# Folding two biases of a feed-forward block into its weight products, and sharing eight copies between two engines

## The chip, the cores and the metric

The kernel runs on one core of a Trainium2 chip. The metric is the device time of one execution in microseconds (us). The core has five kinds of workers that run at the same time and wait for one another through semaphores: TensorE (PE, with its weight loads shown apart as PEld), VectorE (DVE), ScalarE (ACT), GpSimd (POOL), and the queue of SyncE (SP), which issues the transfers (DMA). All data is float32.

## The reference

Four residual steps on tokens x (2 x 1024 x 256) with a context of 2 x 64 x 256. Only the second step changes; the first matters for one detail.

```python
x = x + L0_xattn(layernorm(x), ctx)      # 8 heads of 64, 4 windows; q,k,v products, softmax, Wo, bo
x = x + L0_ffn(layernorm(x))             # below
x = x + L1_xattn(layernorm(x), ctx)      # 16 heads of 16, sigmoid
x = x + L1_ffn(x)                        # soft mixture: logits, two softmaxes, 8 experts, gelu

def L0_ffn(x):                           # 8 groups of 256 tokens, each with its own weights
    xg = x.reshape(8, 256, 256)
    h1 = einsum('gmh,goh->gmo', xg, W1) + b1[:, None, :]     # 1024 wide, no activation
    h2 = einsum('gmo,gho->gmh', h1, W2) + b2[:, None, :]
```

There is nothing between the two products of L0_ffn, and the layernorm has neither scale nor shift, so that the 256 numbers of a normed token add up to zero.

## The kernel before, in words

Tokens stand in four quads of 512 (`xq[q]`, four tiles of 128 rows). Weights of the feed-forward groups come as one tensor `wff`: for each group, on each of 128 partitions, eight rows (oc) of 2 x 256 numbers, W1 beside W2 transposed. `load_group(g)` (L836) reads one group, 2 MB, into one of three buffers `wg`; group 0 comes in five pieces, group 1 in two.

`product(g)` (L852) multiplies the two weights of a group into one 256 x 256 matrix: 16 matmuls (each is two MATMUL instructions in the profile, so 32) into a PSUM bank `pmt`, copied to `mt` (L867). `bias_rows(g)` (L870) makes b1 W2: for groups 0 and 1 on PE with b1 broadcast to 32 columns (`pp`, L878, and one DVE step, L885), for the others as eight sums on DVE (L890). They add up in `b2z`, whose row 0 got b2 by DMA and whose other rows were set to zero. `bias(g)` (L894) multiplies b2z by ones, so that the sum over the partitions stands on all of them (`pbs`, L896), and copies it to `bs` (L898). `norm_ff(q)` (L904) norms a quad (moments on DVE, rstd on POOL at L124 and L125, the scaling `hn` on DVE at L819) and transposes it on PE (L133) with copies to `hT` (L134). `feed_forward(q)` (L908) adds `bs` to the tokens on POOL (L912), multiplies hT by mt (`po`, L918) and adds the result to the tokens on DVE (L925).

Around them stands the first attention: `pk` and `pv` (L991, L1004) make keys and values of the context. The values go from PSUM to a block layout `vblk` in eight copies of 64 x 128 on ACT (L1014). `pwk` (L1025) and `pvw` (L1043) fold keys and values with the projections; their banks come from the same four as pk's and pv's. `weigh(q)` makes scores (`psc`, L1068), maxima (L1078), differences (L1080), exponentials on ACT (L1085), sums and weights (L1087, L1090); `turn_weights` transposes them (`pat`, L1101, copy `atT` on ACT, L1103); `attend` multiplies by the folded values (`po`, L1114) and adds to the tokens (L1122).

The program text gives a priority, not the order: each engine's order is laid out when the kernel is built, from what is ready by a plan of the times, and runs in that order. The calls from L1126 on interleave `weigh`, `attend`, `product`, `bias`, `bias_rows`, `norm_ff` and `feed_forward`. Operations written as `nc.any` get ACT or DVE in that plan. SP's queue holds the loads in one order as well: group 4's load (L841) can start only when the buffer of group 1 has no more readers, and w1s and se (`load_layer1`, the weights of later steps) follow on the same queue.

From about 116 us the second attention runs (L1259 to L1369), then the soft mixture, which the change doesn't touch.

Of the kernel before, what the change touches and what calls it, by code (L numbers as in the profile page):

```python
# [9 lines left out]
FP = mybir.dt.float32  # L10
AF = mybir.ActivationFunctionType
ALU = mybir.AluOpType
# [3 lines left out]
P = 128  # L16
B = 2
S = 1024
D = 256
DC = D // P  # L20
# [13 lines left out]
NG, FF = 8, 1024  # L34
OC = FF // P
# [17 lines left out]
def tile_kernel(  # L53
# [19 lines left out]
    nc = tc.nc  # L73
# [9 lines left out]
    def bank(name, side=0):  # L83
        return ps[side].tile([P, 512], FP, tag="bank", name=name)
# [3 lines left out]
    ones = const.tile([P, P], FP, name="ones")  # L88
# [710 lines left out]
    with (  # L799
# [7 lines left out]
        ggb = w1p.tile([P, 2, D], FP, name="ggb")  # L807

        NCT, NPE = DC * B * NK, DC * NK
        fr = w1p.tile([P, NCT + NPE + NG * OC], FP, name="fr")  # L810
        ctxd = fr[:, 0:NCT].rearrange("p (c b s) -> p c b s", c=DC, b=B)
        pes = fr[:, NCT : NCT + NPE].rearrange("p (c s) -> p c s", c=DC)
        b1s = fr[:, NCT + NPE :].rearrange("p (g c) -> p g c", g=NG)

        def normed(xt, name):
            mv, rstd = moments(xt, name)
            hn = lnp.tile([P, QT, D], FP, tag="hn", name=f"hn_{name}")
            for t in range(QT):
                nc.vector.tensor_scalar(  # L819
                    hn[:, t, :], xt[:, t, :], mv[:, t, 0:1], rstd[:, t : t + 1],  # L820
                    ALU.subtract, ALU.mult,
                )
            return hn

        def layernorm(xt, name, side=0, out=nc.any.tensor_copy):
            hn = normed(xt, name)
            hT = lnp.tile([P, DC, QN], FP, tag="hT", name=f"hT_{name}")
            transposed(hn, hT, name, side, out)
            return hT

        wide = ExitStack()
        wff = wide.enter_context(tc.tile_pool(name="wff", bufs=3))
        ffc = wide.enter_context(tc.tile_pool(name="ffc", bufs=1))
        weights = {}

        def load_group(g, parts=(OC,)):  # L836

            wg = wff.tile([P, OC, 2, D], FP, tag="wg", name=f"wg_{g}")
            i = 0
            for n in parts:  # L840
                nc.sync.dma_start(out=wg[:, i : i + n], in_=wff_in[g, :, i : i + n])  # L841
                i += n
            weights[g] = wg[:, :, 0, :], wg[:, :, 1, :]


        b2z = ffc.tile([P, NG, D], FP, name="b2z")
        bo_bc = ffc.tile([P, D], FP, name="bo_bc")


        mts, bss = [], []  # L850

        def product(g):  # L852
            if g not in weights:
                load_group(g)
            w1g, w2g = weights[g]
            pm = bank(f"pmt_{g}", 1)
            for oc in range(OC):
                for hc in range(DC):
                    nc.tensor.matmul(  # L859
                        pm[:, ts(hc, D)],  # L860
                        lhsT=w1g[:, oc, ts(hc, P)],
                        rhs=w2g[:, oc, :],
                        start=(oc == 0 and hc == 0),
                        stop=(oc == OC - 1 and hc == DC - 1),
                    )
            mt = ffc.tile([P, DC, D], FP, name=f"mt_{g}")
            nc.any.tensor_copy(mt, pm.rearrange("p (c n) -> p c n", c=DC))  # L867
            mts.append(mt)

        def bias_rows(g):  # L870

            acc = b2z[:, g, :]
            if g < 2:

                pp = bank(f"pp0_{g}", 1)
                for oc in range(OC):
                    j = oc % 4
                    nc.tensor.matmul(  # L878
                        pp[ds(32 * j, 32), 0:D],
                        lhsT=b1s[:, g, oc : oc + 1].to_broadcast([P, 32]),  # L880
                        rhs=weights[g][1][:, oc, :],
                        start=(oc < 4),
                        stop=(oc >= 4),
                    )
                nc.vector.scalar_tensor_tensor(  # L885
                    acc, pp[:, 0:D], 1.0 / 32.0, acc, ALU.mult, ALU.add
                )
                return
            for oc in range(OC):
                nc.vector.scalar_tensor_tensor(  # L890
                    acc, weights[g][1][:, oc, :], b1s[:, g, oc : oc + 1], acc, ALU.mult, ALU.add
                )

        def bias(g):  # L894
            pb = bank(f"pbs_{g}", 1)
            nc.tensor.matmul(pb[:, 0:D], lhsT=ones, rhs=b2z[:, g, :], start=True, stop=True)  # L896
            bs = ffc.tile([P, D], FP, name=f"bs_{g}")
            nc.any.tensor_copy(bs, pb[:, 0:D])  # L898
            bss.append(bs)


        hTfs = {}
# [5 lines left out]
        def feed_forward(q, side=0):  # L908
            for i in range(QN // GN):
                g = q * (QN // GN) + i  # L910
                xg = xq[q][:, ts(i, 2), :]
                nc.gpsimd.tensor_tensor(  # L912
                    xg, xg, bss[g].unsqueeze(1).to_broadcast([P, 2, D]), ALU.add
                )
                po = bank(f"po_{g}", side)
                for t in range(2):
                    for dc in range(DC):
                        nc.tensor.matmul(  # L918
                            po[:, ts(t, D)],
                            lhsT=hTfs[q][:, dc, ds(i * GN + t * P, P)],  # L920
                            rhs=mts[g][:, dc, :],
                            start=(dc == 0),
                            stop=(dc == DC - 1),
                        )
                nc.vector.tensor_tensor(  # L925
                    xg, xg, po.rearrange("p (t d) -> p t d", t=2), ALU.add
                )
# [7 lines left out]
        with tc.tile_pool(name="p0", bufs=1) as p0, tc.tile_pool(name="a0", bufs=2) as a0:  # L935

            wk0s = p0.tile([P, DC, H0 * DH0], FP, name="wk0s")
            wv0s = p0.tile([P, DC, H0 * DH0], FP, name="wv0s")
            wq0s = p0.tile([P, C0, D], FP, name="wq0s")
# [6 lines left out]
                nc.sync.dma_start(out=xTs[q], in_=xT[q])  # L946
                nc.sync.dma_start(out=xq[q], in_=x[q])

            nc.gpsimd.memset(b2z, 0.0)
            load_group(0, (1, 1, 2, 2, 2))  # L950
            for t_, s_ in (
                (fr, front), (wk0s, wk0), (wq0s, wq0), (wv0s, wv0), (b2z[0:1], b2.unsqueeze(0)),
                (wo0s, wo0), (bo_bc, bo0.partition_broadcast(P)),
            ):
                nc.sync.dma_start(out=t_, in_=s_)
# [33 lines left out]
            for c in range(C0):  # L989
                for dc in range(DC):  # L990
                    nc.tensor.matmul(  # L991
                        pk[:, ts(c, P)],
                        lhsT=wk0s[:, dc, ts(c, P)],
                        rhs=hcT[:, dc].rearrange("p b j -> p (b j)"),
                        start=(dc == 0),
                        stop=(dc == DC - 1),
# [5 lines left out]
            for c in range(C0):  # L1002
                for dc in range(DC):
                    nc.tensor.matmul(  # L1004
                        pv[:, ts(c, P)],
                        lhsT=wv0s[:, dc, ts(c, P)],
                        rhs=hcT[:, dc].rearrange("p b j -> p (b j)"),
                        start=(dc == 0),
                        stop=(dc == DC - 1),
                    )  # L1010
            for c in range(C0):
                for e in range(2):
                    r = slice(e * DH0, (e + 1) * DH0)
                    nc.scalar.copy(  # L1014
                        vblk[r, c, :, e, :],
                        pv[r, ts(c, P)].rearrange("p (w j) -> p w j", j=KJ),
                    )

            wk = p0.tile([P, DC, NBW, H0 * KJ], FP, name="wk")
            for dc in range(DC):  # L1020
                pws = [bank(f"pwk_{dc}_{e}") for e in range(2)]
                for c in range(C0):
                    for e in range(2):
# [3 lines left out]
                            lhsT=wq0s[r, c, ts(dc, P)],  # L1027
                            rhs=kT[r, c, :],
                            start=True,
                            stop=True,  # L1030
# [8 lines left out]
            for g in range(NBW // 2):  # L1039
                pw = bank(f"pvw_{g}")  # L1040
                for i in range(2):
                    for c in range(C0):
                        nc.tensor.matmul(  # L1043
                            pw[ds(32 * c, 32), ts(i, D)],
                            lhsT=vblk[:, c, 2 * g + i].rearrange("p e j -> p (e j)"),
                            rhs=wo0s[:, c, :],
                            start=True,
                            stop=True,
# [75 lines left out]
                    )  # L1124

            weigh(0)  # L1126
            bias_rows(0)
            product(1)
            turn_weights(0)
            weigh(1)  # L1130
            attend(0)
            product(2)
            bias(0)
            bias_rows(1)
            weigh(2)
            attend(1)
            norm_ff(0)
            product(3)
            bias(1)
            bias_rows(2)  # L1140
            feed_forward(0)
            weigh(3)
            attend(2)
            product(4)
            bias(2)
            bias_rows(3)
            load_layer1()
            norm_ff(1)
            attend(3)
        product(5)  # L1150
        bias(3)
        bias_rows(4)
        feed_forward(1)
        product(6)
        bias(4)
        bias_rows(5)
        norm_ff(2)
        bias(5)
        bias_rows(6)
        feed_forward(2)  # L1160
        bias(6)

        with (
            tc.tile_pool(name="a1c", bufs=1, side="right") as a1c,
# [35 lines left out]
            for c in range(C1):  # L1200
                for dc in range(DC):
                    nc.tensor.matmul(
                        pk[:, ts(c, P)],
                        lhsT=wk1s[:, dc, ts(c, P)],
                        rhs=ctxd[:, dc],
# [82 lines left out]
            norm_ff(NQ - 1)  # L1288
            norm_queries(1)
            norm_queries(2)  # L1290
            bias_rows(7)


            vsum = a1c.tile([P, C1, B], FP, name="vsum")
# [14 lines left out]
                vsum, pvs[:, 0 : C1 * B].rearrange("p (c b) -> p c b", c=C1), 0.5, None, ALU.mult  # L1309
            )  # L1310
            queries(0)
            bias(7)
            turn_slot_rows(0)
            work = ExitStack()
            for q in range(NQ):
# [204 lines left out]
```

## Time and profile before

| what | value |
|---|---|
| median of 3 runs | 430.95 us (430.89 to 431.24) |
| the profiled execution | 430.34 us, of which the span in the profile is 428.6 |
| PE, PEld, DVE, ACT, POOL busy in the span | 421.4, 313.4, 336.9, 111.2, 81.6 us |
| L859, the products of the weights | 256 MATMULs, 57.9 us busy |
| L890, sums of b1 W2 on DVE | 48, 24.5 us busy |
| L896 and L878, bias matmuls on PE | 16 and 32 MATMULs |
| L912, adds of the bias on POOL | 8, 10.4 us busy |
| granted TensorE clock | 1.0 throughout |

A group of the profile is one line, one engine and one operation: tiles written and read, partitions x elements, the number, then busy time, the mean of one in ns, and the idle time of the engine just ahead of them with what ended it. The chain that ended last is followed back from the last instruction, at each step to what released it. Matmuls overlap in the records, so the busy time of PE is more than the work it has; the distance from one start to the next tells the pace.

### The profile page before, as it was taken

Reading aid. Unit: us, or ns where it says so; the run is one execution under the profiler, and the core shown is the slowest. Engines: PE = TensorE matmul, PEld = TensorE weight load, DVE = VectorE, ACT = ScalarE, POOL = GpSimd, SP = SyncE. Lnnn points to the kernel's source line nnn. Section 1 sums busy time; section 2 is a strip of 40 time slices with the busy share of each in tenths; the row PEclk is TensorE's granted clock in tenths of the full one; section 3 lists DMA queues with packets and bytes.
Section 4 is the critical chain, followed back from the end, with each engine's and each line's share of the span. In section 5 each row is a group of like instructions: output and inputs, shape, how many; then the busy total and the mean of one; then the engine's idle time right before and its main releaser. Section 6 shows DMA issues by size and latency. Waiting matters only on the chain.

```text
span 428.6 us, 6368 instructions
## 1 busy us (share of the span) xinstructions
PE 421.4 (98%) x2318; PEld 313.4 (73%) x2318; DVE 336.9 (79%) x753; ACT 111.2 (26%) x210; POOL 81.6 (19%) x83
## 2 busy tenths in 40 slices
PE   8999999999999999999999999999999999999997
PEld 7788797888644445444478844799998874499996
DVE  0587989899767788997768989995994489785956
ACT  1212224203444431433570455400000003520000
POOL 3012232225212220200975920000000000000000
PEclk9999999999999999999999999999999999999999
DMA  8997695420462431321043663551012665620002
GB/s 275 401 419 314 242 377 203 186 98 2 154 197 99 81 44 29 45 30 21 0 161 148 114 96 58 79 81 20 0 38 76 134 116 89 97 44 1 2 2 98
DMA packets 99281, 50.03 MB, mean 117 GB/s; under 512 B 87857, under 2 KB 94385, under 8 KB 97841
## 3 DMA queue, kind: packets, MB, share of 16 engines
q1 hardware_dynamic: 99250, 49.63, 41.5%
q8 instruction: 18, 0.29, 0.3%
q14 instruction: 13, 0.11, 0.1%
HBM read 32.74 MB, written 6.30 MB: 91 GB/s over the span
## 4 chain that ended last, share of the span: by engine, by line
PE 79%; DVE 13%; SPq 2%; DMA 2%; issue 1%; ACT 1%; POOL 1%; DVEq 0%; ACTq 0%
PE psl L409 13%; PE pc L586 12%; PE pp L586 11%; PE pmh L511 10%; PE pmt L859 9%; PE pl L256 7%; PE pq L1259 3%; PE po L918 2%; DVE b2z L890 2%; SPq L158 2%; PE pf L1273 2%; PE psg L1329 1%; PE poT L1361 1%; DMA wg<-in_wff_dram 1%; DVE lg L264 1%
## 5 line engine op out<-in xcount | busy, mean ns | idle before, releaser
L859 PE MATMUL pmt<-wg 128*128 128x256 f32 x256 | 57.9, 382 | 0.4 <-DMA wg<-in_wff_dram 0.4
L409 PE MATMUL psl<-xh,lg 128*128 128x258 f32 x256 | 56.8, 380 | 0.0
L256 PE MATMUL pl<-seT,xhT 128*128 128x512 f32 x128 | 56.1, 594 | 0.2 <-DVE rmax L275 0.2
L859 PEld LDWEIGHTS pmt<-wg 128*128 128x128 f32 x256 | 48.5, 192 | 7.3 <-DMA wg<-in_wff_dram 0.8
L409 PEld LDWEIGHTS psl<-xh,lg 128*128 128x128 f32 x256 | 48.2, 190 | 7.4 <-issue 0.5
L256 PEld LDWEIGHTS pl<-seT,xhT 128*128 128x128 f32 x128 | 24.1, 190 | 29.2 <-issue 25.7
L395 POOL TENSOR_TENSOR lg<-lg,mb 128x1024 f32<-128x1024 f32 x13 | 33.2, 2607 | 26.8 <-ACT mb L203 25.3
L586 PEld LDWEIGHTS pp<-ms,mh 128*128 128x128 f32 x256 | 29.4, 192 | 1.3 <-issue 0.7
L586 PE MATMUL pp<-ms,mh 128*128 128x128 f32 x256 | 30.0, 276 | 0.1
L279 ACT ACTIVATE ec<-lg,nm 128x1024 f32<-128x1024 f32 x16 | 18.4, 1149 | 39.8 <-DVE nm L264 39.8
L890 DVE SCALAR_TENSOR_TENSOR b2z<-wg,fr,b2z 128x256 f32<-128x256 f32 x48 | 24.5, 513 | 0.3
L521 ACT ACTIVATE mh<-mh 128x512 f32<-128x512 f32 x32 | 19.2, 627 | 20.8 <-DVE mh L557 19.2
L511 PE MATMUL pmh<-slT,ms 128*128 128x512 f32 x48 | 24.2, 592 | 0.0
L586 PE MATMUL pp<-m_sums,mh 128*128 128x128 f32 x192 | 22.1, 275 | 0.0
L586 PE MATMUL pc<-pr,ec 128*128 128x128 f32 x192 | 22.1, 275 | 0.0
L586 PEld LDWEIGHTS pp<-m_sums,mh 128*128 128x128 f32 x192 | 21.8, 192 | 0.0
L586 PEld LDWEIGHTS pc<-pr,ec 128*128 128x128 f32 x192 | 21.8, 192 | 0.0
L1338 ACT ACTIVATE sg<-psg 128x512 f32<-128x512 f32 x32 | 16.5, 603 | 18.6 <-PE psg L1329 18.6
L398 ACT ACTIVATE lg<-lg 128x1024 f32<-128x1024 f32 x16 | 16.1, 1045 | 18.0 <-POOL lg L395 18.0
L308 DVE STREAM_TRANSPOSE tr<-ec 128x512 f32<-128x512 f32 x32 | 19.8, 674 | 0.0
L597 DVE TENSOR_TENSOR mh<-mh,mh 128x1024 f32<-128x1024 f32 x16 | 18.5, 1216 | 0.5 <-PE pp L586 0.5
L586 PE MATMUL pc<-pr_sums,ec 128*128 128x128 f32 x160 | 18.5, 275 | 0.0
(196 smaller groups left out, 679.2 us busy)
## 6 DMA issues: line engine op xcount, KB each, us to landing
wg<-in_wff_dram SPq DMA_DIRECT2D x6, 2048.0 KB, 14.1
ec<-tr SPq DMA_DIRECT2D x128, 64.0 KB, 2.3
xT<-in_xT_dram SPq DMA_DIRECT2D x4, 512.0 KB, 13.4
x<-in_x_dram SPq DMA_DIRECT2D x4, 512.0 KB, 15.9
wg<-in_wff_dram SPq DMA_DIRECT2D x2, 1024.0 KB, 11.1
d_a<-tr_a SPq DMA_DIRECT2D x4, 512.0 KB, 2.7
hTa<-d_a SPq DMA_DIRECT2D x16, 128.0 KB, 3.0
xhT<-tr_m SPq DMA_DIRECT2D x64, 32.0 KB, 2.0
```

Of the source, the lines that this page charges most:

```text
L256: nc.tensor.matmul(pl, lhsT=xhTs[q][:, dc, ts(t, P)], rhs=in_order(seT[:, n], dc), start=(dc == 0), stop=(dc == DC - 1),)
L279: nc.scalar.activation(ecs[q][:, :, t, :], lg.rearrange("p (h n) -> p h n", h=2), AF.Exp, bias=nm[:, 1:2], scale=-1.0, accum_out=zcs[b][:, ...
L308: ins = nc.vector.transpose(tr[:, :, :, t, :].rearrange("p r c n -> p c r n"), half[:, t, :].rearrange("p (c r n) -> p c r n", c=EC // 2, ...
L395: engine.tensor_tensor(lgs[b][s], lgs[b][s], mbs[b], ALU.add)
L409: nc.tensor.matmul(pz[:, 0:XW], lhsT=lgs[b][s][:, ts(c, P)], rhs=xhs[b * QB + s // QT][:, s % QT, :], start=(s == 0), stop=(s == ST - 1),)
L511: nc.tensor.matmul(to, lhsT=lefts[i][:, ts(j, P)], rhs=in_order(slTs[b][0], i) if i < 2 else rights[b][i], start=True, stop=True,)
L521: nc.scalar.activation(h, h, AF.Gelu)
L586: nc.tensor.matmul(to, lhsT=left(k, m), rhs=right[:, k, :], start=(k == 0), stop=(k == QT - 1),)
L597: nc.vector.tensor_tensor(dst, x, y, op)
L859: nc.tensor.matmul(pm[:, ts(hc, D)], lhsT=w1g[:, oc, ts(hc, P)], rhs=w2g[:, oc, :], start=(oc == 0 and hc == 0), stop=(oc == OC - 1 and hc ...
L890: nc.vector.scalar_tensor_tensor(acc, weights[g][1][:, oc, :], b1s[:, g, oc : oc + 1], acc, ALU.mult, ALU.add)
L1338: nc.scalar.activation(sg[:, j, :], psgs[j], AF.Tanh, scale=0.5 * DH1**-0.5)
```

## The change

Since the numbers of a normed token add up to zero, its first number is minus the sum of the others. So hn W1' = sum over j >= 1 of hn_j (W1_j - W1_0). The first column of W1 is then free, and so is the first number of the token. The host lays b1 into W1's first column and moves the real first column to a place behind W2 (a row is now 513 numbers). On the chip the new `prepare(g)` subtracts that column from columns 1 to 255 of W1, in place, and the first number of each normed token is set to one. The product of the weights then has b1 W2 in its first row, b2 is added to that row, and the matmul of the tokens brings both biases along. `prepare` runs on DVE for group 0 and on ACT for the others, where the column is negated first so that it can serve as a bias. It is called at the end of the product of the group before and loads the group if that was not done.

The calls of `bias_rows` and `bias`, the add of `bs` to the tokens, and the zeroing of b2z are gone. Half of the eight copies of the first attention's values go to DVE.

```diff
-        def normed(xt, name):
+        def normed(xt, name, skip=0):
...
-                    hn[:, t, :], xt[:, t, :], mv[:, t, 0:1], rstd[:, t : t + 1],
+                    hn[:, t, skip:], xt[:, t, skip:], mv[:, t, 0:1], rstd[:, t : t + 1],
...
         def layernorm(xt, name, side=0, out=nc.any.tensor_copy):
-            hn = normed(xt, name)
+            hn = normed(xt, name, 1)
+            nc.gpsimd.memset(hn[:, :, 0:1], 1.0)
...
-            wg = wff.tile([P, OC, 2, D], FP, tag="wg", name=f"wg_{g}")
+            wg = wff.tile([P, OC, 2 * D + 1], FP, tag="wg", name=f"wg_{g}")
...
-            weights[g] = wg[:, :, 0, :], wg[:, :, 1, :]
+            weights[g] = wg[:, :, 0:D], wg[:, :, D : 2 * D], wg[:, :, 2 * D :]
-        b2z = ffc.tile([P, NG, D], FP, name="b2z")
+        b2r = ffc.tile([1, NG, D], FP, name="b2r")
...
+        def prepare(g):
             if g not in weights:
                 load_group(g)
+            w1g, _, first = weights[g]
+            less = ffc.tile([P, OC], FP, name=f"less_{g}")
+            for part, scalar in enumerate((g > 0, g > 0)):
+                ocs = range(part * OC // 2, (part + 1) * OC // 2)
+                some = slice(ocs.start, ocs.stop)
+                if scalar:
+                    nc.scalar.activation(less[:, some], first[:, some, 0], AF.Copy, scale=-1.0)
+                for oc in ocs:
+                    w = w1g[:, oc, 1:]
+                    if scalar:
+                        nc.scalar.activation(w, w, AF.Identity, bias=less[:, oc : oc + 1])
+                    else:
+                        nc.vector.tensor_scalar(w, w, first[:, oc, :], None, ALU.subtract)
+
+        def product(g):
+            if g == 0:
+                prepare(0)
...
             nc.any.tensor_copy(mt, pm.rearrange("p (c n) -> p c n", c=DC))
+            nc.gpsimd.tensor_tensor(mt[0:1, 0, :], mt[0:1, 0, :], b2r[:, g, :], ALU.add)
             mts.append(mt)
+            if g + 1 < NG:
+                prepare(g + 1)
-        def bias_rows(g):
...
-        def bias(g):
...
             for i in range(QN // GN):
...
-                nc.gpsimd.tensor_tensor(
-                    xg, xg, bss[g].unsqueeze(1).to_broadcast([P, 2, D]), ALU.add
-                )
...
-            nc.gpsimd.memset(b2z, 0.0)
...
-                    nc.scalar.copy(
+                    (nc.vector.tensor_copy if e else nc.scalar.copy)(
                         vblk[r, c, :, e, :],
```

More of the change, by code (lines that the diff above doesn't have):

```diff
@@ L809, in tile_kernel @@
         NCT, NPE = DC * B * NK, DC * NK
-        fr = w1p.tile([P, NCT + NPE + NG * OC], FP, name="fr")
+        fr = w1p.tile([P, NCT + NPE], FP, name="fr")
         ctxd = fr[:, 0:NCT].rearrange("p (c b s) -> p c b s", c=DC, b=B)
-        pes = fr[:, NCT : NCT + NPE].rearrange("p (c s) -> p c s", c=DC)
-        b1s = fr[:, NCT + NPE :].rearrange("p (g c) -> p g c", g=NG)
-        def normed(xt, name):
+        pes = fr[:, NCT:].rearrange("p (c s) -> p c s", c=DC)
+        def normed(xt, name, skip=0):
             mv, rstd = moments(xt, name)
@@ L842, in load_group @@
                 i += n
-            weights[g] = wg[:, :, 0, :], wg[:, :, 1, :]
-        b2z = ffc.tile([P, NG, D], FP, name="b2z")
+            weights[g] = wg[:, :, 0:D], wg[:, :, D : 2 * D], wg[:, :, 2 * D :]
+        b2r = ffc.tile([1, NG, D], FP, name="b2r")
         bo_bc = ffc.tile([P, D], FP, name="bo_bc")
-        mts, bss = [], []
-        def product(g):
+        mts = []
+        def prepare(g):
             if g not in weights:
                 load_group(g)
-            w1g, w2g = weights[g]
+            w1g, _, first = weights[g]
[14 more added lines that the diff above has]
+                prepare(0)
+            w1g, w2g, _ = weights[g]
             pm = bank(f"pmt_{g}", 1)
@@ L867, in product @@
             nc.any.tensor_copy(mt, pm.rearrange("p (c n) -> p c n", c=DC))
+            nc.gpsimd.tensor_tensor(mt[0:1, 0, :], mt[0:1, 0, :], b2r[:, g, :], ALU.add)
             mts.append(mt)
-        def bias_rows(g):
[L872 to L883, printed above, removed]
-                    )
[L885 to L892, printed above, removed]
-        def bias(g):
[L895 to L899, printed above, removed]
+            if g + 1 < NG:
+                prepare(g + 1)
         hTfs = {}
@@ L911, in feed_forward @@
                 xg = xq[q][:, ts(i, 2), :]
-                nc.gpsimd.tensor_tensor(
-                    xg, xg, bss[g].unsqueeze(1).to_broadcast([P, 2, D]), ALU.add
-                )
                 po = bank(f"po_{g}", side)
@@ L947, in load_quad @@
                 nc.sync.dma_start(out=xq[q], in_=x[q])
-            nc.gpsimd.memset(b2z, 0.0)
             load_group(0, (1, 1, 2, 2, 2))
             for t_, s_ in (
-                (fr, front), (wk0s, wk0), (wq0s, wq0), (wv0s, wv0), (b2z[0:1], b2.unsqueeze(0)),
+                (fr, front), (wk0s, wk0), (wq0s, wq0), (wv0s, wv0), (b2r, b2.unsqueeze(0)),
                 (wo0s, wo0), (bo_bc, bo0.partition_broadcast(P)),
@@ L1126, in tile_kernel @@
             weigh(0)
-            bias_rows(0)
             product(1)
@@ L1132, in tile_kernel @@
             product(2)
-            bias(0)
-            bias_rows(1)
             weigh(2)
@@ L1138, in tile_kernel @@
             product(3)
-            bias(1)
-            bias_rows(2)
             feed_forward(0)
@@ L1144, in tile_kernel @@
             product(4)
-            bias(2)
-            bias_rows(3)
             load_layer1()
@@ L1150, in tile_kernel @@
         product(5)
-        bias(3)
-        bias_rows(4)
         feed_forward(1)
         product(6)
-        bias(4)
-        bias_rows(5)
         norm_ff(2)
-        bias(5)
-        bias_rows(6)
         feed_forward(2)
-        bias(6)
         with (
@@ L1290, in tile_kernel @@
             norm_queries(2)
-            bias_rows(7)
             vsum = a1c.tile([P, C1, B], FP, name="vsum")
@@ L1311, in tile_kernel @@
             queries(0)
-            bias(7)
             turn_slot_rows(0)
@@ L1477 @@
     ctxT = a["ctx_1024"].reshape(B * NK, D).T
-    b1 = a["L0_ffn_b1"].reshape(NG, P, OC).transpose(1, 0, 2)
+    w1f, w2f = a["L0_ffn_W1"], a["L0_ffn_W2"].transpose(0, 2, 1)
     gammas = _np.stack([a["L1_ffn_gamma_x"], a["L1_ffn_gamma_slot"]])
@@ L1482 @@
         ("xT", a["x"].reshape(NQ, QN, DC, P).transpose(0, 3, 2, 1)),
-        ("front", flat(by_row(ctxT), by_row(pe.T), b1)),
+        ("front", flat(by_row(ctxT), by_row(pe.T))),
         ("wq0", by_row(a["L0_xattn_Wq"].T)),
@@ L1490 @@
             "wff",
-            _np.stack(
-                [a["L0_ffn_W1"], a["L0_ffn_W2"].transpose(0, 2, 1)], axis=2
-            ).reshape(NG, P, OC, 2, D),
+            _np.concatenate(
+                [a["L0_ffn_b1"][:, :, None], w1f[:, :, 1:], w2f, w1f[:, :, :1]], axis=2
+            ).reshape(NG, P, OC, 2 * D + 1),
         ),
```

## The prediction

> **What bounds the kernel now.** I read the page's busy line first, then the PE timeline with its gaps, then the chain that ended last, then the groups by form for the prices.
>
> The busy line:
>
> ```profile
> PE 421.4 (98%) x2318; PEld 313.4 (73%) x2318; DVE 336.9 (79%) x753; ACT 111.2 (26%) x210; POOL 81.6 (19%) x83
> ```
>
> A PE that is busy 98% of the time need not be at its peak, since its records overlap: a product matmul has a mean of 382 ns, yet 32 of them in a row take 6.91 us, 216 ns each. So I looked for gaps. Up to 150 us the PE timeline has only these that are longer than 0.1 us, beside the first 1.04 us (columns: start, length, line, operation, and in brackets the idle time before it with what ended it):
>
> ```profile
> 7.05 5.45 PE L859 MATMUL pmt<-wg 128*128 128x256 f32 x24 [0.44 <-DMA wg<-in_wff_dram]
> ...
> 19.57 1.16 PE L1025 MATMUL pwk<-kT,wq0s 64*128 64x128 f32 x14 [1.00 <-ACT vblk L1014]
> ...
> 51.63 0.65 PE L133 MATMUL pt_f<-ident,hn_f 128*128 128x128 f32 x4 [0.60 <-DVE e L1080]
> ...
> 67.18 1.13 PE L1114 MATMUL po<-vw,atT 128*128 128x256 f32 x4 [0.52 <-DVE x L925]
> ```
>
> The chain says the same from the end backwards (columns: start, length, what). From 67.18 to 149.2 it is PE alone, piece joined to piece, and the pieces that this change deletes stand in it:
>
> ```profile
> 14.28 1.00 PE pp L878 x16
> ...
> 68.31 5.61 PE pmt L859 x26
> 73.92 0.43 PE pbs L896 x2
> 74.35 0.87 PE pt_f L133 x8
> 75.22 0.44 PE pat L1101 x4
> 75.66 0.87 PE pmt L859 x4
> ```
>
> From 35.5 to 67.2 the chain runs over DVE, in good part over the L890 sums, but PE has only the 0.60 and 0.52 us gaps there and runs at its 216 ns pitch between them: two engines are close to equal, and both are relieved. After 150 us the kernel is unchanged, its PE stream again almost without gaps, so what is won ahead of it should be kept.
>
> The Trainium skill ("Trainium Kernel Development and Optimization", Performance Expectations) calls matmul busy time a bad metric and judges by LDWEIGHTS busy and MFU; LDWEIGHTS is 73% here. By that alone up to 27% of PE could be slack that hides the deletion; the pitch of 216 ns without gaps speaks against it, and it comes back as a rival.
>
> **Part by part.** Prices:
>
> ```profile
> L890 DVE SCALAR_TENSOR_TENSOR b2z<-wg,fr,b2z 128x256 f32<-128x256 f32 x48 | 24.5, 513 | 0.3
> ...
> L1085 ACT ACTIVATE e<-e,rstd_a 128x128 f32<-128x128 f32 x16 | 5.1, 390 | 18.1 <-DVE e L1080 18.1
> ...
> L1176 ACT ACTIVATE sq<-se 128x256 f32<-128x256 f32 x8 | 3.3, 417 | 0.2
> ...
> L1014 ACT COPY vblk<-pv 64x128 f32<-64x128 f32 x8 | 2.1, 259 | 4.3 <-PE pv L1004 4.2
> ...
> L980 DVE TENSOR_SCALAR wq0s<-wq0s,wqm 128x256 f32<-128x256 f32 x4 | 1.1, 347 | 0.0
> ```
>
> 1. bias(g) goes: eight pbs products of two MATMULs, 0.43 us each in the chain: **-3.45** of PE. Its eight bs copies (1.9 us ACT, 1.2 DVE) were hidden.
>
> 2. bias_rows goes: for groups 0 and 1, 16 MATMULs each, 1.00 us each: **-2.0** of PE. For groups 2 to 7, 48 L890 sums, 24.5 us of DVE. That is no time by itself, since PE ran beside it, but it is what made DVE late at the 0.60 and 0.52 gaps: L890 sums stand between mx and e, and between the two L925 adds. The POOL adds of L912 (8, 1315 ns) go too; beside them DVE slows (four hn_a take 4.24 us from 100.63, four others 1.38). With some 12 us of DVE work out of 35 to 67 us and about 3 us less PE work up to there, I take both gaps as gone: **-1.1** (bounds 0 and -1.1). What is late next is PE itself.
>
> 3. vblk on two engines: eight copies take 2.16 us on ACT from 17.36; four on each engine take about 1.07. DVE idles from 16.7 to 18.39, so its half is free. PE would wait until 18.43 rather than 19.53 and comes at 18.57: the gap goes, **-1.0** (bounds 0, if DVE's half is behind other work, and -1.0).
>
> 4. prepare(0): eight DVE subtractions of 128x255 in front of the first product, each after its piece of W has landed. Nearest row L980, 347 ns, same form, 256 wide; the two-input L890 is the dear end, 513. DVE idles until 10.63 (hcT waits for a transfer), so nothing is queued behind. PE needs 0.865 us for each eighth and DVE 0.35, so only the first after the third piece shows: 0.35 plus a hop of 0.1: **+0.45** (0.35 to 0.65).
>
> 255 is odd. The Trainium skill ("VectorE: DVE Perf Modes", What auto-detection actually checks) lets a one-source SBUF operation run at two elements a cycle only if the outermost counts are even, or equal; equal they are, so by it the 347 holds. The row bears the double rate out (L980 347, the two-input ggb product of the same size 414, though L980 has a pointer scalar more). Lost, it would cost 0.13 us at the start and 0.13 on each of 16 hn_f, off PE's path.
>
> 5. prepare(1) to (7): per group two copies of 128x4 (taken at 0.2, between the 0.19 of a 128x1 read and the 0.26 of vblk) and eight ACT Identities of 128x255 with a pointer bias. L1085 (pointer, 128 wide) takes 390; ACT copies of 512 and 256 take 586 and 380, 0.8 ns a column; so 390 + 127 x 0.8 = 492 ns, and 0.4 pitch, as L1085's four in 1.28 us overlap by 0.09. A group is 3.6 us, seven are 25 us on an ACT that is busy 38 us of the first 115. PE takes 6.91 us for a product and needs only the first eighth at its start. Group 1 lands in halves at 22.5 and 25.0; PE comes at about 24.7; ACT has the first eighth by 23.2. Group 2 lands at 32.4, ready from 33.1, PE comes at about 35. Group 3 lands at 40.0, PE at about 44. So the new wait costs 0 by these figures. What stands behind a waiting Identity on ACT: vblk, the exponentials, the atT, hT and mt copies, and PE waits for each of them. Bounds 0 to +2.0 (seven products, with waits like those that the PE timeline has now, 0.3 each on a mean); I take **+0.4**.
>
> 6. The loads of groups 4 to 7 move ahead, to the end of the product before, past load_layer1's four transfers on SP's queue. Now they wait there for pp L878 (18.3 us) and for b2z L890 (19.4); then for a product alone, so group 4 goes out at about 32 instead of 45.6. w1s and se follow or go before; se was first read at 59.1. Cost 0.
>
> 7. Rows of 2052 bytes instead of 2048, 0.2% more bytes; the first pieces bound the start (the 0.44 gap), and the third value weights, wv0s, land at 14.6 where PE will want them at about 14.7. I take **+0.2** (0 to 0.7: a tenth of the 7 us in which the third piece comes).
>
> The Trainium skill ("DMA: Bandwidth & Descriptors", How a descriptor splits into AXI transactions) speaks against this part: off a 256-byte boundary, bytes below the start are fetched too, and a remainder is a transaction of its own. By it, an estimate, 2052 bytes take 65 to 73 beats where 2048 took 64, and the third piece 1 to 7% more; the sum would lose about 0.3 instead of 0.2.
>
> 8. POOL: 8 adds on one partition, 256 wide, about 0.65 each (half of L912), and four memsets of 0.1, against 10.4 + 1.8 removed. The add waits for the mt copy, and rstd's pow stands behind it; L912 waited in the same way for bs. mt is read by L918 a product or more later. Cost 0; without that cover up to 0.7 once.
>
> Sum: -3.45 - 2.0 - 1.1 - 1.0 + 0.45 + 0.4 + 0.2 = **-6.5 us**. The profiled execution took 430.34 (428.6 of it the span): 423.8. The median of the runs is 0.6 above that execution, so **424.4**.
>
> **Rivals.**
> - *ACT hands back part.* With 25 us more on ACT, copies that PE waits for come late, or products wait at their start; 2.0 instead of 0.4, and the vblk and DVE gaps stay as they are (2.1): -2.8, 428.1. For: all copies of mt, atT and hT are on ACT. Against: ACT idles 50.6 us ahead of mt copies alone.
> - *PE had slack* (the busy rule above): then only waits go, not PE work: -1.1 - 1.0 + 1.05 = -1.05, about 430. Against: the pitch.
> - *Slower: group 1's Identities queue ahead of vblk on ACT.* They come earlier in the program. If ACT's order has them first, vblk waits from 17.4 to about 28 (the second half of the group lands at 25.0, 1.9 us of work, then the copies), 10 us at pwk and pvw with nothing else for PE: -6.5 + 10 = +3.5, 434.5. It decides at whether the order places them before 17.4. Against: now PE's order did not put product(1) into the 1.00 us gap at 18.6, so group 1 was not counted on there; and ACT's slot squares (program order: far later) run at 59.1, as se lands, ahead of earlier steps: what is ready goes first.
> - *All covers hold* (parts 5 and 7 cost nothing): -7.1, 423.8, within the forecast's range.
>
> **Chances.** Forecast with the last case 0.70, ACT hands back part 0.17, PE had slack 0.06, slower 0.07. A measurement tells 0.2% (0.9 us) from no change: faster 0.87, same 0.05, slower 0.08. The range takes the forecast's bounds and the first rival: 422.8 to 428.2.
>
> **What would show it.** PE instructions down by 48 MATMULs; PE busy down by some 6; no gap by vblk, e or x; L859's first gap about 0.9 us instead of 0.44; the last stages as long as before. Wrong if ACT rows (Identity) stand as releasers of pmt for more than 2 us, if L859's pitch leaves 216 ns (weights at odd word offsets), or if the wait by vblk grows.

## The result and the profile after

| | before | after |
|---|---|---|
| median of 4 runs each | 430.92 us (430.5 to 431.24) | 426.93 us (426.77 to 427.07) |
| profiled execution, span in it | 430.34, 428.6 us | 426.77, 424.7 us |

The ratio is 0.9908, 95% interval 0.9891 to 0.9925: 4.0 us faster, where 6.5 were forecast (424.4, range 422.8 to 428.2). The sign and the range hold; 2.5 us of the gain are missing, and the question is where they went.

The busy line of the page after:

```profile
PE 416.5 (98%) x2270; PEld 310.4 (73%) x2270; DVE 317.3 (75%) x714; ACT 131.6 (31%) x269; POOL 74.5 (18%) x86
```

PE has lost 48 instructions, as many as forecast, and 4.9 us of busy time. DVE has lost 19.6 us and ACT gained 20.4. The PE timeline after, up to 50 us, shows where PE waits now (columns: start, length, line, operation, in brackets the idle time before it and what ended it):

```profile
7.38 5.45 PE L879 MATMUL pmt<-wg 128*128 128x256 f32 x24 [0.50 <-DVE wg L870]
...
16.33 2.05 PE L1013 MATMUL pwk<-kT,wq0s 64*128 64x128 f32 x24
19.10 1.16 PE L1013 MATMUL pwk<-kT,wq0s 64*128 64x128 f32 x8 [0.72 <-DVE wk L1022]
20.19 3.66 PE L1031 MATMUL pvw<-wo0s,vblk 128*32 128x256 f32 x64
...
25.66 7.41 PE L879 MATMUL pmt<-wg 128*128 128x256 f32 x32
...
38.81 7.18 PE L879 MATMUL pmt<-wg 128*128 128x256 f32 x32 [1.79 <-ACT wg L868]
45.83 1.95 PE L1056 MATMUL psc<-wk,xT 128*128 128x128 f32 x16
```

The 0.60 and 0.52 us gaps of before are gone. The 1.00 us gap ahead of pwk's last part has become 0.72, though pwk started 0.87 earlier. And there is a gap that before did not have: product(2), at 38.81, waits 1.79 us for ACT. The chain that ended last names the same place, and product(1) before it (its longest pieces: start, length, what). It leaves PE for DVE's differences and ACT's exponentials, and PE's product stands behind them; product(1) waits in the same way for its second half.

```profile
27.38 1.28 ACT e L1073 x4
29.35 3.72 PE pmt L879 x16
33.51 1.80 PE psc L1056 x16
36.84 1.28 ACT e L1073 x4
38.81 7.18 PE pmt L879 x32
```

Reading the same work in both PE timelines, start against start, gives a ledger. A start that moves by another amount than the one above it tells what the stretch between them won or lost.

| PE starts | before | after | difference | what the stretch did |
|---|---|---|---|---|
| product(0), 3rd piece on | 7.05 | 7.38 | +0.33 | start later: prepare(0) and longer rows |
| pwk | 17.20 | 16.33 | -0.87 | a pp product of 1.00 gone |
| pvw | 20.66 | 20.19 | -0.47 | vblk stage 0.40 longer, not 1.0 shorter |
| product(1) | 26.14 | 25.66 | -0.48 | nothing |
| product(2) | 37.00 | 38.81 | +1.81 | product(1) 0.34 longer, the gap 1.79, joints 0.16 |
| psc of quad 2 | 45.43 | 45.83 | +0.40 | pp and one pbs gone; product 0.11 longer |
| first feed_forward | 58.60 | 57.56 | -1.04 | pbs and the 0.60 gap gone |
| second feed_forward | 84.75 | 82.04 | -2.71 | pbs and the 0.52 gap gone |
| first psg | 114.80 | 110.59 | -4.21 | the other pbs gone |
| pl after its wait for rmax | 185.56 | 181.36 | -4.20 | nothing |
| the span's end | 428.6 | 424.7 | -3.9 | a new gap of 0.39 at 245.99 |

So the losses sit in three places: vblk (1.4 against the forecast), product(1) and (2) behind ACT (2.2, where 0.4 was forecast), and a small late one (0.4). The start (0.3 less than forecast) and the deletions (0.7 more) give 1.0 of that back, which leaves the 2.5 that are missing.

One row of the ledger is weaker than it looks. Up to the third piece of product(0), PE's work is the same in before, e5 and e6 (the piece starts at 6.68 to 7.06), and again in after and the seven other experiments (7.33 to 7.71). These starts scatter by 0.4, so that the +0.33 of this one pair, near the low end, cannot be told from the forecast's +0.65; the two groups are about 0.6 apart on a mean.

### The profile page after: what moved, and what is told of

It is laid out like the page before. It is cut to its first block, busy times and chain, and to the rows that moved or that the text cites. A ratio compares the mean times of both kernels' runs of the same rounds, so it can differ in the third digit from the quotient of the medians.

```text
span 424.7 us, 6297 instructions
## 1 busy us (share of the span) xinstructions
PE 416.5 (98%) x2270; PEld 310.4 (73%) x2270; DVE 317.3 (75%) x714; ACT 131.6 (31%) x269; POOL 74.5 (18%) x86
## 4 chain that ended last, share of the span: by engine, by line
PE 86%; DVE 8%; ACT 1%; issue 1%; DMA 1%; POOL 1%; SPq 0%; DVEq 0%; ACTq 0%
PE psl L409 13%; PE pmt L879 12%; PE pc L586 12%; PE pp L586 11%; PE pmh L511 10%; PE pl L256 7%; PE pq L1233 3%; PE po L907 3%; PE pf L1247 3%; PE psg L1301 2%; PE psc L1056 2%; PE poT L1333 2%; DVE lg L264 1%; PE po L1102 1%; DMA wg<-in_wff_dram 1%
## 5 line engine op out<-in xcount | busy, mean ns | idle before, releaser
L879 PE MATMUL pmt<-wg 128*128 128x256 f32 x256 | 58.4, 383 | 2.4 <-ACT wg L868 1.8
L256 PE MATMUL pl<-seT,xhT 128*128 128x512 f32 x128 | 56.1, 594 | 0.2 <-DVE rmax L275 0.2
L879 PEld LDWEIGHTS pmt<-wg 128*128 128x128 f32 x256 | 48.2, 191 | 10.2 <-ACT wg L868 2.7
L256 PEld LDWEIGHTS pl<-seT,xhT 128*128 128x128 f32 x128 | 24.1, 190 | 29.2 <-issue 25.7
L395 POOL TENSOR_TENSOR lg<-lg,mb 128x1024 f32<-128x1024 f32 x13 | 33.2, 2585 | 27.2 <-ACT mb L203 25.3
L868 ACT ACTIVATE wg<-wg,less 128x255 f32<-128x255 f32 x56 | 23.4, 495 | 0.1
L545 ACT COPY mh<-pmh 128x512 f32<-128x512 f32 x8 | 4.6, 569 | 50.2 <-PE pmh L511 50.2
## 6 DMA issues: line engine op xcount, KB each, us to landing
wg<-in_wff_dram SPq DMA_DIRECT2D x6, 2052.0 KB, 13.9
```

Source lines behind the costliest of these rows:

```text
L256: nc.tensor.matmul(pl, lhsT=xhTs[q][:, dc, ts(t, P)], rhs=in_order(seT[:, n], dc), start=(dc == 0), stop=(dc == DC - 1),)
L395: engine.tensor_tensor(lgs[b][s], lgs[b][s], mbs[b], ALU.add)
L868: nc.scalar.activation(w, w, AF.Identity, bias=less[:, oc : oc + 1])
L879: nc.tensor.matmul(pm[:, ts(hc, D)], lhsT=w1g[:, oc, ts(hc, P)], rhs=w2g[:, oc, :], start=(oc == 0 and hc == 0), stop=(oc == OC - 1 and hc ...
```

## The experiments

Theory: the deletions are worth what was forecast; two things give part of it back, the sharing of the vblk copies, which brings nothing, and ACT's order, which puts ready weights behind exponentials that still wait. The main rivals: the sharing does help and something else made the stage longer; the 25 us of new ACT work cost by their amount; PE had slack, so that the deletions are worth less. Each experiment was timed beside the kernel before on one chip (431.1 us for e1 to e4, 430.7 for e5 to e8, 430.97 for e9); after stood beside 430.92. So a difference between an experiment and after of a few tenths of a us is within what separates the chips.

### e1 and e2: all copies of the values on ACT again, and in two copies instead of eight

```diff
-                    (nc.vector.tensor_copy if e else nc.scalar.copy)(
+                    nc.scalar.copy(
```

> The changed kernel with all eight vblk copies on ACT again. Theory (the two engines take turns on the copies, so sharing gains nothing): the copies end at about 18.65 us of the span, before pwk's last eight can end, where the shared ones end at 19.37; pvw starts 0.3 to 0.4 us earlier, and the time falls from 426.9 to about 426.5. Rival (sharing halves the stage, and what is missing was lost elsewhere): the time rises by about 1.0 to 427.9.

```diff
-            for c in range(C0):
-                for e in range(2):
...
+            for e in range(2):
+                r = slice(e * DH0, (e + 1) * DH0)
+                nc.scalar.copy(
+                    vblk[r, :, :, e, :].rearrange("p c w j -> p (c w) j"),
+                    pv[r].rearrange("p (v j) -> p v j", j=KJ),
+                )
```

> The changed kernel with the vblk copies as two of 64x512 on ACT in place of eight of 64x128 on two engines. Theory (the length of the copies sets the gap at pwk; taking turns is why sharing did not shorten it): two copies of 0.58 us end at about 17.6, the pwk gap of 0.72 goes and pvw starts about 0.8 us earlier: 426.1. Rival (something else, wk's copies or a transfer, holds pvw): 426.9, no change.

Measured: e1 426.34, ratio 0.9894 [0.9877, 0.9910]; e2 425.06, ratio 0.9863 [0.9848, 0.9878], both against 431.1 on their chip. Taking the sharing out again costs nothing (0.6 less than after, and the intervals overlap); with merged copies the time is 1.9 us under after, where 0.8 was expected. The reason is in the timelines. First after, ACT:

```profile
16.50 0.26 ACT L1002 COPY vblk<-pv 64x128 f32<-64x128 f32 x1 [3.04 <-PE pv L992]
17.12 0.26 ACT L1002 COPY vblk<-pv 64x128 f32<-64x128 f32 x1 [0.36 <-DVE vblk L1002]
...
```

and DVE's half in the same kernel:

```profile
16.79 0.30 DVE L1002 COPY vblk<-pv 64x128 f32<-64x128 f32 x1
17.41 0.29 DVE L1002 COPY vblk<-pv 64x128 f32<-64x128 f32 x1 [0.32 <-ACT vblk L1002]
...
18.35 0.69 DVE L1022 COPY wk<-pwk 128x512 f32<-128x512 f32 x1
19.08 0.29 DVE L1002 COPY vblk<-pv 64x128 f32<-64x128 f32 x1
```

The two engines never copy at the same time. Each waits 0.32 to 0.36 us for the other, every step; a pair takes 0.62, more than two copies in a row on ACT. The last of DVE's copies then falls behind a copy of wk. So the eight end at 19.37, while e1, whose pv ends 0.21 later, has them in one run of 2.16 us by 18.87:

```profile
16.71 2.16 ACT L1002 COPY vblk<-pv 64x128 f32<-64x128 f32 x8 [3.04 <-PE pv L992]
```

From pwk's start to pvw's start e1 needs 3.46 us, as before did, where after needs 3.86. In e2 two copies take 1.17 us, and pwk goes through without a gap (PE's timeline of e2):

```profile
16.60 2.55 PE L1012 MATMUL pwk<-kT,wq0s 64*128 64x128 f32 x32
19.07 3.66 PE L1030 MATMUL pvw<-wo0s,vblk 128*32 128x256 f32 x64
```

pvw starts 1.12 earlier than after, and that is what the merging is seen to bring; another 0.39 comes from the late gap (below), which e2 does not have. Together that is the 1.5 us by which its span is shorter (423.2).

### e5: before, with nothing but the sharing

```diff
-                    nc.scalar.copy(
+                    (nc.vector.tensor_copy if e else nc.scalar.copy)(
```

> The kernel before with only the vblk copies shared between ACT and DVE. Theory (turns): no gain, pvw starts up to 0.5 us later, 430.9 to 431.4. Rival (sharing is worth the 1.0 us of the gap, as the forecast had it): 429.9.

Measured: 431.16 against 430.7, ratio 1.0015 [1.0004, 1.0026]. Alone, too, the sharing wins nothing; by the medians it loses 0.46 us. From pwk's start to pvw's start it needs 4.02 us, 0.56 more than before, and pvw starts at 21.31 (20.66 before), behind a gap that ends with DVE's copy of wk (PE's timeline of e5):

```profile
20.22 1.16 PE L1025 MATMUL pwk<-kT,wq0s 64*128 64x128 f32 x8 [0.88 <-DVE wk L1034]
```

### e9: the values made twice, in two PSUM banks

That the engines take turns is seen; why is not. They write the same tile and read the same bank. Here PE makes the values a second time into a bank of its own (1.8 us more PE work), ACT copies from one bank and DVE from the other, into the same vblk.

```diff
-            pv = bank("pv0")
+            pvs0 = [bank("pv0"), bank("pv0b", 1)]
+            for pv in pvs0:
...
-                        pv[r, ts(c, P)].rearrange("p (w j) -> p w j", j=KJ),
+                        pvs0[e][r, ts(c, P)].rearrange("p (w j) -> p w j", j=KJ),
```

> The changed kernel with the values made twice, into two PSUM banks, 16 MATMULs more (1.8 us of PE); ACT copies from the one and DVE from the other, into the same vblk. Theory (the two engines take turns because they read one bank): no copy waits for the other engine, four copies end about 1.2 us after the first, the pwk gap goes, pwk and its wait shrink by 1.4, so that the time is 426.9 + 1.8 - 1.4 = 427.3. Rival (they take turns because they write one tile, or DVE's half is late anyway): the waits of 0.36 stay and the time is 428.5 or more.

Measured: 426.08, ratio 0.9888 [0.9872, 0.9905]. ACT's four copies, in the timeline of e9:

```profile
16.62 0.75 ACT L1003 COPY vblk<-pv 64x128 f32<-64x128 f32 x4 [3.04 <-PE pv L993]
```

and DVE's four:

```profile
18.34 0.92 DVE L1003 COPY vblk<-pv0b 64x128 f32<-64x128 f32 x4 [1.63 <-PE pv0b L993]
```

Four in a row on each engine. In the program ACT's second copy still comes behind DVE's first; if the shared target made it wait, ACT would have stood until 18.34 and later, and it was done at 17.37. So it is the shared source that makes them take turns, not the shared target. (In e9 the source is another tile as well as another bank; which of the two the waits go by is not told apart.) And pvw starts at 20.22, as early as after (20.19), although PE had 1.8 us more to do. (As DVE's bank was filled later, the two did not copy at the same moment here; that they can is not shown.) The total came out better than the 427.3 expected: product(1) takes 7.08 and product(2) waits 1.45 in place of 7.41 and 1.79, as ACT's exponentials and Identities fall differently there.

### e3 and e4: ACT's order mended, and the new ACT work left out

e3 keeps all the work and ties the exponentials of quads 0 and 1 behind the Identities of groups 1 and 2. e4 leaves the subtraction out for groups 1 to 7, and with it part of what is computed.

```diff
+                        last[g] = nc.scalar.activation(
+                            w, w, AF.Identity, bias=less[:, oc : oc + 1]
+                        ).ins
...
+                with tc.issue_after(last[q + 1]) if q < 2 else ExitStack():
```

> The changed kernel with one thing else: on ACT the exponentials of the first two quads stand behind the Identities of groups 1 and 2, which needs no new wait for data. Theory (the 1.79 us in front of product(2) and the 0.3 inside product(1) come from ACT's order, Identities behind exponentials that wait for DVE): both go, 426.9 - 2.1 = 424.8. Rival (group 2 lands too late, or ACT has too much work): the gap in front of product(2) stays over 1 us and the time within 0.5 of 426.9, or the late exponentials cost as much.

```diff
-                    nc.scalar.activation(less[:, some], first[:, some, 0], AF.Copy, scale=-1.0)
+                    continue
```

> The changed kernel without the subtraction for groups 1 to 7 (the column of W1 is not taken off, so that part of the computation is left out). Theory (ACT's 25 us of Identities cost only the waits at products 1 and 2): 426.9 - 2.2 = 424.7, the same as with the order mended. Rival (they cost more all along, by late copies of mt, atT and hT): under 424.

Measured: e3 424.40, e4 424.44, each with a ratio of 0.9849 [0.9834, 0.9864]. Order alone brings back as much as leaving the work out, with which ACT's busy time falls from 131.6 to 107.7 us. ACT's timeline after shows the trouble:

```profile
33.59 0.59 ACT L1091 COPY atT<-pat 128x512 f32<-128x512 f32 x1
36.84 1.28 ACT L1073 ACTIVATE e<-e,rstd_a 128x128 f32<-128x128 f32 x4 [2.66 <-DVE e L1068]
38.03 0.29 ACT L864 ACTIVATE less<-wg 128x4 f32<-128x4 f32 x2
38.26 3.29 ACT L868 ACTIVATE wg<-wg,less 128x255 f32<-128x255 f32 x8
```

The weights of group 2 had landed by 32.1. ACT was idle for 2.66 us, from 34.18 to 36.84, waiting for DVE's differences, because its order has the exponentials first; only then come the ten steps that PE waits for. In e3 they go into that hole:

```profile
34.06 0.32 ACT L865 ACTIVATE less<-wg 128x4 f32<-128x4 f32 x2
34.31 3.29 ACT L869 ACTIVATE wg<-wg,less 128x255 f32<-128x255 f32 x8
37.51 1.26 ACT L1077 ACTIVATE e<-e,rstd_a 128x128 f32<-128x128 f32 x4
```

and PE's product(1) and product(2) in e3 follow without a wait:

```profile
25.98 7.08 PE L882 MATMUL pmt<-wg 128*128 128x256 f32 x32
...
36.85 7.07 PE L882 MATMUL pmt<-wg 128*128 128x256 f32 x32
```

The exponentials of the second quad now start 0.67 us later than after, and no gap on PE comes of it. Group 1 gains in the same way: its second half is worked on from 24.96, as soon as it has landed, where after had it behind the exponentials, from 28.79.

### e6: before, without any of the two biases

To price the deletions alone, all calls of bias_rows and bias and the add of bs are taken out of before. Both biases are left out of what is computed.

```diff
-            bias_rows(0)
...
-            bias(0)
-            bias_rows(1)
...
-                nc.gpsimd.tensor_tensor(
-                    xg, xg, bss[g].unsqueeze(1).to_broadcast([P, 2, D]), ALU.add
-                )
```

> The kernel before without bias_rows, bias and the adds of bs (both biases of the feed-forward are left out). Theory (PE is the bound, so its deleted 5.45 us and the two DVE gaps of 1.1 count in full): 430.9 - 6.5 = 424.4, at most 0.5 off for other small gaps. Rival (PE had slack): 429 to 430.

Measured: 424.17 against 430.7, ratio 0.9852 [0.9839, 0.9865]: -6.5 us. Steps 1 and 2 had -3.45 - 2.0 - 1.1 = -6.55. PE had no slack to hide the deleted work. The close agreement is in part luck: e6 also pays the late gap (0.53), and PE has come to L256 at 178.60 there, 6.96 earlier than before (185.56). Of that 0.37 is an earlier third piece (6.68), and a new wait of 0.38 for wv0s, at 14.29, goes against it. So the deletions brought about 0.4 more than their pieces, as in the ledger.

### e8: half of each subtraction on DVE

```diff
-            for part, scalar in enumerate((g > 0, g > 0)):
+            for part, scalar in enumerate((False, g > 0)):
```

> The changed kernel with the first half of each group's subtraction on DVE, the second on ACT as before. Theory (order, not amount of work, makes the wait): DVE's half of group 2 is ready early or late by where it stands among DVE's steps; ACT's second half still stands behind the exponentials but is needed 3.5 us later, so the gap of 1.79 falls under 0.5: 425.3 to 425.8. Rival (the amount on ACT counts): the same gain of 1 to 2 us, but spread over later products, with a gap at product(2) still over 1 us.

Measured: 427.67 (427.23 to 429.68), ratio 0.9941 [0.9924, 0.9958]. The expectation missed by 2 us, and the rival's gain did not come either: the time is 0.7 above after. The profiled execution was its longest (429.68, clock 0.995, pvw 5.35 us there instead of 3.66), so only the two waits are read from it, in the PE timeline:

```profile
29.07 7.18 PE L879 MATMUL pmt<-wg 128*128 128x256 f32 x32 [1.04 <-DVE wg L870]
...
41.43 7.17 PE L879 MATMUL pmt<-wg 128*128 128x256 f32 x32 [1.24 <-DVE wg L870]
```

Both products wait for DVE now. For product(2) DVE's half starts at 41.03, behind the differences of the next scores at 39.23 and an add to the tokens at 39.84. Four steps take 1.13 us there, where ACT needs 1.70, but the trouble moved with the work: DVE's order has the scores' work first as well. (product(1) stands right behind the long pvw, so its 1.04 may not be in the other executions; what makes the time 0.7 longer than after's is not shown.)

### e7: both mends together

e2's two copies and e3's order in one kernel.

> The changed kernel with both mends: two vblk copies of 64x512 on ACT, and the exponentials of the first two quads behind the Identities of groups 1 and 2. Theory (the two are apart in time and add up): 426.9 - 0.8 - 2.1 = 424.0. Rival (the first mend only moves PE up to the next wait, for the Identities of group 1): 424.8.

Measured: 422.73 (422.55 to 423.2) against 430.7, ratio 0.9823 [0.9811, 0.9836]: 8.0 us faster than before and 4.2 faster than after. That is 1.3 better than the 424.0 expected, which had 0.8 for the merged copies and 2.1 for the order. By the medians the two mends alone brought 1.87 and 2.53, 0.2 more than both together; reckoned against the before of each chip they are 2.05 and 2.71 against 3.98, 0.8 more. So they add up, but only to within that. The PE timeline of e7 has neither gap:

```profile
16.28 2.55 PE L1015 MATMUL pwk<-kT,wq0s 64*128 64x128 f32 x32
...
35.10 7.07 PE L882 MATMUL pmt<-wg 128*128 128x256 f32 x32
```

## Why the prediction was right, and where its size was off

The sign and the main term held with their mechanism. Two smaller steps, 3 and 5, had the mechanism wrong, and both misses made the kernel slower. That the time still lies in the range is owed to the range's upper end, which was taken from a rival, and it would lie 0.7 higher but for a gain that was not forecast (below).

**Steps 1 and 2** (deletions, -6.55) held: e6 measures -6.5 with the late gap in it, and the ledger has the pp and pbs pieces and both gaps gone. The rival that PE had slack falls with it. The Trainium skill ("Trainium Kernel Development and Optimization", Performance Expectations) calls matmul busy time a bad metric; here both shares, 98% and 73%, stood beside a PE without slack for the deleted work (e6), and the pitch of 216 ns without gaps was what told it.

**Step 3** (vblk on two engines, -1.0) failed. It took two halves of four copies as parallel and checked only that DVE was idle. It was not asked whether the two can read pv together. They take turns, a pair in 0.62 us; the stage grew by 0.40. Missed by 1.4 us.

The Trainium skill ("PSUM — Partial Sum Buffer", PSUM bank collisions raise a hardware error) says that two engines may not touch the same group of 32 partitions of one bank at once, and that semaphores have to keep them apart, where different groups of one bank may be used at the same time. The two halves here lie on partitions 0 to 63 and 64 to 127, so by the page they could have run together, and the turns would come from the program's own waits. The runs show turns on one bank and none on two (e9), and the profile names the other engine's copy as what ended each wait; copies from one bank without these waits were not tried, so what the chip itself would allow stays open.

**Step 4 and step 7** (start, +0.45 and +0.2) came to +0.33 together in the profiled pair; over all kernels with either start it is about 0.6, so the sum of 0.65 is not contradicted. The subtraction takes 351 ns (groups by form, after, up to 190 us; count, then busy us and mean ns, then idle time ahead):

```profile
L870 DVE TENSOR_SCALAR wg<-wg 128x255 f32<-128x255 f32 x8 | 2.6, 351 | 7.0 <-DMA wg<-in_wff_dram 7.0
...
L868 ACT ACTIVATE wg<-wg,less 128x255 f32<-128x255 f32 x56 | 23.4, 495 | 0.1
...
L888 POOL TENSOR_TENSOR mt<-mt,b2r 1x256 f32<-1x256 f32 x8 | 5.8, 728 | 27.4 <-ACT mt L887 14.6 <-DMA b2r<-in_b_dram 11.1 <-DVE mt L887 1.7
```

That is 4 ns over the 347 of the even width: an odd 255 does not lose the 0.13 us that was feared. The Trainium skill ("VectorE: DVE Perf Modes", What auto-detection actually checks), cited in the prediction, had it so. The six loads of a whole group land 13.9 us (median) after their issue, 14.1 before; the two first pieces of group 0 take 3.1, and 2.9 before. No price of the 2052-byte rows can be told from that. The rule of the Trainium skill ("DMA: Bandwidth & Descriptors", How a descriptor splits into AXI transactions), cited in the prediction, made the sum 0.1 dearer; no run here shows it at this size. (The prediction's 65 to 73 beats in place of 64 are 2 to 14% more, not its 1 to 7%.)

**Step 5** (ACT, +0.4 of 0 to +2.0) had the price right and the place wrong. An Identity takes 495 ns where 492 was worked out, a `less` 0.20. But the sentence "Group 2 lands at 32.4, ready from 33.1" took landing as the start, as if ACT took what is ready. It asked what stands behind an Identity on ACT, and not what stands ahead of it. ACT's order is fixed when the kernel is built, and it had the exponentials first, which waited for DVE until 36.84. The same happened in small to the second half of group 1 (product(1) 7.41 for 7.07). It cost 2.2 in the ledger and 2.5 by e3 and e4: 1.8 to 2.1 more than taken, and just above the upper bound. That bound was built of small waits at seven products; what came was one large wait, at one of them. For groups 3 to 7 the figures held, with no wait on ACT. (The 38 us that the prediction gives for ACT's work in the first 115 us of before are too many, the trace has 27.7; the slip is on the safe side, and idle time was not what was lacking.)

**Steps 6 and 8** held at 0: no product waits for a transfer after the first, and POOL's adds, 728 ns instead of 650, end no wait of PE.

**Not foreseen:** the 0.39 us late gap (below). Against it stand about 0.7, net, by which the stretches of the ledger with deletions won more than the deleted pieces and gaps: 0.2 up to pwk, 0.5 after 45 us. I put it down to the joints between pieces; that was not tested, but e6 shows some tenths of the same kind.

**The sum again:** +0.33 - 6.55 + 0.40 + 2.24 + 0.39 - 0.7 = -3.9, the difference of the spans. Of the rivals, "ACT hands back part" (428.1) described the mechanism that came, with its price of about 2 right; it was also right that the vblk gap stays, and went too far in keeping the DVE gaps, which are gone. "Slower" did not come: ACT's order had the vblk copies ahead of group 1's Identities; but what it feared, work ahead of other work in a fixed order, did come one group later.

Of the signs that the prediction named, the 48 MATMULs fewer and the pitch of 216 ns came; PE's busy time fell by 4.9 instead of some 6, L859's first gap (now L879) is 0.50 and not 0.9, and the gap by vblk stayed at 0.72. Two of its signs of being wrong came in substance: ACT's Identities held pmt up for 1.79 us as a gap and 0.34 inside product(1), and the stage by vblk grew, though its gap did not.

## What to carry to other kernels

When a step moves to an idle engine, look up what that engine's order has ahead of it, and when *that* can start: ready data and idle time are no cover if the instruction ahead waits. Before two engines share copies, look whether they read one PSUM bank; in that case fewer and wider copies on one engine won here (1.17 us for two against 2.16 for eight), and the sharing nothing. And when a gain falls short, list the same PE instruction's start in both timelines: the stretch where the difference jumps is the one to test.

## What the runs showed of the hardware beyond this

Late in the kernel, the first of DVE's two L498 takes 1.40 us where it took 1.10 before, and PE waits for it (PE timeline, after):

```profile
245.99 2.22 PE L511 MATMUL pmh<-sl_sums,m_sums 128*128 128x512 f32 x4 [0.39 <-DVE sl_sums L498]
```

The gap is in after, e1, e3 (0.21), e4 (0.34), e6 (0.53), e7 (0.43), e8 (0.50) and e9, and neither in before nor in e2 and e5. e6 has none of the added operations, so the change's work is not needed for it. What goes with it in all eleven traces is POOL: its adds at L395 still run when L498 starts (DVE's timeline, then POOL's, after):

```profile
244.44 1.40 DVE L498 TENSOR_TENSOR sl_sums<-slT 128x512 f32<-128x512 f32 x1
```

```profile
230.70 14.59 POOL L395 TENSOR_TENSOR lg<-lg,mb 128x1024 f32<-128x1024 f32 x5 [1.95 <-DMA mb<-mrow]
```

The two overlap for 0.48 us in e5, 0.54 in before, 0.85 in after and 1.00 in e6, and L498 takes 1.02, 1.10, 1.40 and 1.55 us. In every trace it ends 0.54 to 0.56 us after POOL's last add, wherever it started. The second L498, at about 350 us with nothing on POOL, takes 0.69 in every trace. So L498 hardly gets on while POOL adds, and how far ahead of POOL's end it starts decides on PE's gap (none at 0.54, 0.21 at 0.68, 0.53 at 1.00). The change seems to have made that gap only by bringing L498 to another moment beside POOL. It fits the slowdown of DVE beside POOL that the prediction read from L912. The two were not run beside each other by design, and why they hinder each other is not shown.
